# Moving two chunks of the shared expert's gate and up products into the last sequence's cross-attention of a decoder layer, with two smaller changes of order

## The chip, the cores and the metric

The kernel runs on one core of one Trainium2 chip. The metric is the device time of one execution in microseconds (us), as the median of several runs. All arithmetic is in 32-bit floats.

## The reference, cut to what matters

A decoder layer is applied to x of 8 sequences with 112 tokens and 512 features. Three blocks follow one another, each on a layer-normalised x and added to x:

```python
x = x + attn(layernorm(x), W_K, W_Q, W_V, W_O)       # 16 heads of 128, causal
x = x + xattn(layernorm(x), ctx_2048, Wq, Wk, Wv)    # 32 heads of 16, context of 375 per sequence
x = x + ffn(layernorm(x), gate_w, expert_*, shared_*)

# xattn: q = rmsnorm(x @ Wq.T by head), k = rmsnorm(ctx @ Wk.T by head), v = ctx @ Wv.T
#        out = softmax(q k^T / sqrt(16)) v
# ffn:   probs = softmax(x @ gate_w.T); the best 2 of 8 experts per token, their weights normed
#        out  = (silu(x @ shared_gate.T) * (x @ shared_up.T)) @ shared_down.T      # 704 wide
#        out += sum over the 2 experts e: w_e * (silu(x @ gate_e.T) * (x @ up_e.T)) @ down_e.T   # 352 wide
```

## The kernel before

The 896 tokens are held as 7 tiles of 128 rows (`xs`), with sequences 1 to 7 in the first 112 rows of a tile each and sequence 0 spread over the last 16 rows of all seven. The kernel has three stages, in this order: self-attention in four groups of heads, cross-attention, and the feed-forward part.

Code is traced in the order in which it stands, and a planner then gives each engine its own order. An engine runs its queue strictly in that order. The planner takes what stands first among the instructions that it holds to be ready, by costs of its own, so an instruction can float ahead of code that is written before it. Two helpers hold it: `tc.issue_after(i)` queues what is traced under it, on the engine of `i`, behind `i`; `tc.keep_in_program_order(i)` queues `i` behind what is already traced on its engine. Neither makes an engine wait for a result.

**Cross-attention before its loop.** `project_k` makes the raw keys of sequence 0. Seven tiles of x are normalised (`ln_apply`), projected to queries (`project_q`) and normed by head (`normed_q`). `project_q` ends in `head_squares`, a squaring on GpSimd (POOL, L407) and a sum on VectorE (DVE, L408). `normed_q` takes the square root on ScalarE (ACT, `rms_scale`, L411), multiplies on DVE (L523), turns the tile on TensorE (PE, L526) and copies it back on ACT (L527). `spread_q` (DVE, L533, two instructions per sequence) makes the operand of the scores from it. Two other jobs of POOL lie here: `weight_sums` (L454, four sums `wt` of weight blocks, the last two written into the query weights) and `chunk_sums(1)` (L471, four small sums of the next sequence's context). Both feed a product of 2 x 2 blocks with seven in place of eight multiplications (`first_chunks`, PE L476).

**The loop of cross-attention.** It runs over 8 sequences b, 2 halves of the heads cp and 3 thirds of the context m. `exp_scores` issues the scores of one (b, cp, m) into the four buffers of the PSUM pool `sc` (PE L569, tile `xs`) and four exponentials (ACT L577, tile `e`). `weigh` multiplies the exponentials of a half with the values (PE L594, tile `pv`), one half later. `attend(t)` turns and divides the result of a finished sequence and adds it to x. Between these, for b below 7, stand the products for the keys and values of sequence b+1. At the end of an iteration `spread_q`, `rms_scale` and `normed_k` (PE L551, ACT L554, tile `kT`) prepare b+1. Here `rms_scale` is held behind the exponentials of (b, 1, 1), so on ACT it stands between those and the exponentials of (b, 1, 2). Square root and exponential use different tables of ACT, and a load of the table (ACT_TABLE_LOAD) stands before the first instruction with another one. In iteration 5 the first four tiles of x, finished by then, are normalised and turned into `xn3`, the operand of the feed-forward part.

**The feed-forward part.** `shared_chunk(i, half, w)` makes 128 of the 704 gate and up rows (chunk i of 6) for half of the tokens: PE L722 (tile `gu`; gate and up are 8 matmul records each of 448 columns; chunk 5 has one such product), ACT L728 (Silu) and DVE L729. Its order is chunk (0, 0), the last three tiles of `xn3`, chunk (1, 0), `route`, and then the other ten. `route` computes the two experts of each token on DVE; POOL scatters the normalised rows to DRAM (L884), and `rows_of` loads them back sorted by expert (L914). 18 steps of experts follow, and `finish` adds the shared expert's down product. The weights of the shared expert are three tiles `sw`, two chunks in each, in the pool `weights` with three buffers, which the query, key and value weights of cross-attention hold before.

Of the kernel before, what the change touches and what calls it, by code (L numbers as in the profile page):

```python
# [15 lines left out]
F32 = mybir.dt.float32  # L16
I32 = mybir.dt.int32
AF = mybir.ActivationFunctionType
ALU = mybir.AluOpType
AX = mybir.AxisListType  # L20

P = 128
B, S, D = 8, 112, 512
NT = B * S
TT = NT // P
SP = P - S
ND = D // P
HALF = NT // 2
# [48 lines left out]
def decoder_layer(  # L77
    ctx: ExitStack, tc: tile.TileContext, x, ctxT, wqk, wv_all, wo, wx, wgate, wsgu, wsd, wegu, wed_a, wed_b, consts, out
):
    nc = tc.nc  # L80
# [6 lines left out]
    wpool = ctx.enter_context(tc.tile_pool(name="weights", bufs=3))  # L87
    mm = ctx.enter_context(tc.tile_pool(name="mm", bufs=4, space=PSUM))
# [28 lines left out]
    def psum(pool, name):  # L117
        return pool.tile([P, 512], F32, tag=pool.name, name=name)

    def load_w(pool, src, name):  # L120
        t = pool.tile([P, 4, 512], F32, tag="w", name=name)
        nc.sync.dma_start(out=t, in_=src)
        return t

    def load_ctx(b):
        t = ctxpool.tile([P, ND, M], F32, name=f"ctx{b}", tag="ctx")
        with tc.issue_after(first_weights):
            nc.sync.dma_start(out=t, in_=ctxT[b])
        return t


    def ln_begin(name):
# [251 lines left out]
    with ExitStack() as xa:  # L384
# [19 lines left out]
        def head_squares(n, dst, sums):  # L404

            sq = krp.tile([P, 512], F32, tag="sq", name="sq", bufs=2)
            nc.gpsimd.tensor_tensor(sq[:n], dst, dst, ALU.mult)  # L407
            nc.vector.tensor_reduce(sums, sq[:n].rearrange("p (h d) -> p h d", h=XH), AX.X, ALU.add)  # L408

        def rms_scale(t):  # L410
            nc.scalar.activation(t, t, AF.Sqrt, bias=eps_rms[: t.shape[0]], scale=1.0 / XD)  # L411
            nc.vector.reciprocal(t, t)
# [38 lines left out]
        def weight_sums(which):  # L451
            sums = ((wxv[:, 0:2], wxk[:, 0:2]), (wxv[:, 2:4], wt[0]), (wxv[:, 2:4], wxv[:, 0:2]), (wxk[:, 2:4], wt[1]))
            for i in which:
                nc.gpsimd.tensor_tensor(wt[i], *sums[i], ALU.subtract)  # L454
# [7 lines left out]
        def chunk_sums(b, which):  # L462
            a11, a12, a21, a22 = blocks(b)
            sums = (
                (a21, a22, ALU.add),
                (csum[0], a11, ALU.subtract),
                (a11, a21, ALU.subtract),
                (a12, csum[1], ALU.subtract),
            )
            for i in which:  # L470
                nc.gpsimd.tensor_tensor(csum[i], *sums[i])  # L471
# [30 lines left out]
        def project_q(t):  # L502
            q = qp.tile([P, 512], F32, tag="q", name="q")
            ss = qp.tile([P, XH], F32, tag="qss", name="qss")
            ps = psum(mm, "q")
            for c in range(ND):
                nc.tensor.matmul(
                    ps,
                    xn2[:, c, t * P : (t + 1) * P],
                    wxq[:, c, :],  # L510
                    start=(c == 0),
                    stop=(c == ND - 1),
                )
            nc.scalar.copy(q, ps)
            head_squares(P, q, ss)
            rawq[t] = (q, ss)

        def normed_q(t):

# [21 lines left out]
        def normed_k(b):  # L541
            k, kss = rawk.pop(b)
            keys[b] = kvp.tile([P, ND, M], F32, tag="kT2", name="kT2")
            for m in range(NM):
                k3 = k[:, m, :].rearrange("p (h d) -> p h d", h=XH)
                nc.vector.tensor_tensor(
                    k3, k3, kss[:, m, :, None].to_broadcast([MC, XH, XD]), ALU.mult
                )
                pt = psum(mm, "kT")
                for c in range(ND):  # L550
                    nc.tensor.transpose(  # L551
                        pt[:, c * MC : (c + 1) * MC], k[:, m, c * P : (c + 1) * P], ident[:MC, :MC]
                    )
                nc.scalar.copy(  # L554
                    keys[b][:, :, m * MC : (m + 1) * MC],
                    pt[:, : ND * MC].rearrange("p (c s) -> p c s", c=ND),
                )

        last_exp = {}

        def exp_scores(b, cp, m):

# [66 lines left out]
        new_keys(0)  # L629
        for m in range(NM):  # L630
            project_k(0, m)
        weight_sums((0, 1))
        for lo, hi in ((0, 4), (4, TT)):
            rs2 = ln_rstd(mv2, lo, hi)
            for t in range(lo, hi):
# [2 lines left out]
                    project_q(t - 1)  # L638
                if t >= 2:
                    normed_q(t - 2)  # L640
        project_q(TT - 1)
        normed_q(TT - 2)
        project_v(0, 0)
        rms_scale(rawk[0][1].rearrange("p m h -> p (m h)"))
# [2 lines left out]
        normed_q(TT - 1)  # L647
        spread_q(0)
        project_v(0, 2)
        weight_sums((2, 3))  # L650
        ctxs[1] = load_ctx(1)
        chunk_sums(1, range(4))

        pending = None
        for b in range(B):
            for cp in range(2):
                es = []
                for m in range(NM):
                    es.append(exp_scores(b, cp, m))
                    if m == 0 and pending is not None:  # L660
                        weigh(*pending)

                    if m == 1 and cp == 0 and b >= 2:
                        attend(b - 2)
                    if b + 1 < B:
                        if cp == 0:
                            if m == 0:
                                new_keys(b + 1)
                                pairs = first_chunks(b + 1)
                            next(pairs)  # L670
                        elif m == 0:
                            project_k(b + 1, 2)
                            if b + 2 < B:
                                ctxs[b + 2] = load_ctx(b + 2)
                                chunk_sums(b + 2, range(3))
                        elif m == 1:
                            project_v(b + 1, 2)
                        else:
                            next(pairs)
                            if b + 2 < B:  # L680
                                chunk_sums(b + 2, (3,))
                pending = (b, cp, es)
            if b + 1 < B:
                spread_q(b + 1)

                with tc.issue_after(last_exp[(b, 1, 1)].ins):
                    if b == 5:
                        rs3 = ln_rstd(mv3, 0, 4)
                    rms_scale(rawk[b + 1][1].rearrange("p m h -> p (m h)"))
                normed_k(b + 1)  # L690
                if b == 5:
                    for t in range(4):
                        ln_apply(mv3, rs3, t, xn3)
# [7 lines left out]
    with ExitStack() as ff:  # L701
# [5 lines left out]

        hidden = shp.tile([P, 6, NT], F32, name="hidden")
        wex = ep.tile([P, E, ND, 2 * FF], F32, name="wex")

        def load_shared(i):

            w = load_w(wpool, wsgu[i], f"sw{i}")
            return w.rearrange("p c (i k f) -> p c i k f", i=2, k=2)

        def shared_chunk(i, half, w):
            cols = bass.ds(half * HALF, HALF)
            both = []
            for k, pool in ((0, mm), (1, sc))[: 2 if i < 5 else 1]:
                ps = psum(pool, "gu")  # L720
                for c in range(ND):
                    nc.tensor.matmul(  # L722
                        ps[:, :HALF], w[:, c, i % 2, k, :], xn3[:, c, cols], start=(c == 0), stop=(c == ND - 1)
                    )
                both.append(ps[:, :HALF])
            g = gp.tile([P, HALF], F32, tag="g", name="g")
            if i < 5:
                nc.scalar.activation(g, both[0], AF.Silu)  # L728
                nc.vector.tensor_tensor(hidden[:, i, cols], g, both[1], ALU.mult)  # L729
                return  # L730


            n = P // 2
            gate, up = both[0][:n], both[0][n:]
            low = min(4 * P - half * HALF, HALF)
            nc.scalar.activation(g[:n, :low], gate[:, :low], AF.Silu)
            nc.vector.tensor_tensor(
                hidden[:n, i, half * HALF : half * HALF + low], g[:n, :low], up[:, :low], ALU.mult
            )
            if low < HALF:  # L740
                nc.scalar.activation(g[n:, low:], gate[:, low:], AF.Silu)
                nc.vector.tensor_tensor(hidden[n:, i, 4 * P :], g[n:, low:], up[:, low:], ALU.mult)
# [269 lines left out]
                    nc.vector.tensor_tensor(xs[t][:, cols], p[:, cols], xs[t][:, cols], ALU.add)  # L1012
                    nc.sync.dma_start(out=out[t * P : (t + 1) * P, cols], in_=xs[t][:, cols])

        sw = [load_shared(i) for i in range(3)]
        for e in range(E):
            nc.sync.dma_start(out=wex[:, e], in_=wegu[e])
        rs3b = ln_rstd(mv3, 4, TT)
        rs3s = [rs3] * 4 + [rs3b] * (TT - 4)
        shared_chunk(0, 0, sw[0])  # L1020
        for t in range(4, TT):
            ln_apply(mv3, rs3b, t, xn3)
        for t in range(6):
            normed_row(t)
        shared_chunk(1, 0, sw[0])
        at, share, expert = route()
        for i, half in ((0, 1), (1, 1), *((i, half) for i in range(2, 6) for half in range(2))):
            shared_chunk(i, half, sw[i // 2])

        thirds = [wpool.tile([P, 4, 512], F32, tag="w", name=f"wd{i}") for i in range(3)]  # L1030
# [117 lines left out]
```

## Time and profile before

| | |
|---|---|
| median of 3 runs | 1028.39 us (1027.58 to 1028.48) |
| profiled execution, its own time | 1028.71 us |
| its span, first to last instruction | 1026.9 us |
| PE busy in the span | 999.3 us, 97% |
| DVE, ACT, POOL busy | 39%, 27%, 24% |
| granted TensorE clock, mean | 0.998 |
| chain that ended last, PE's share | 91% |

All times inside the profile count from the start of its span; what lies outside the span is 1.8 us. A busy PE need not be at its peak: the records' ends are modelled, and a matmul that runs at a lower clock is as busy as another. So what PE loses is read from three things: its waits, the distance between the starts of equal matmuls, and the granted clock of a stretch.

| stretch, us | what runs | length, us | PE busy, us |
|---|---|---|---|
| 0 to 450.60 | load, self-attention | 450.6 | 437.8 |
| 450.60 to 506.85 | cross-attention up to the first scores | 56.25 | 53.33 |
| 506.85 to 740.83 | loop, sequences 0 to 6 | 233.98 | 229.15 |
| 740.83 to 762.05 | loop, sequence 7, up to the last turning | 21.22 | 20.11 |
| 762.05 to 834.33 | shared gate and up, routing | 72.28 | 72.28 |
| 834.33 to 983.00 | experts | 148.67 | 148.16 |
| 983.00 to the end | shared down, sums, output | 43.9 | 38.48 |

### The profile page before, as it was taken

How to read it: one execution, taken by the hardware profiler on the slowest of the kernel's cores; microseconds unless marked ns; L12 is line 12 of the kernel's file. 1: busy time of each engine (PE TensorE's matmuls, PEld its weight loads, DVE VectorE, ACT ScalarE, POOL GpSimd, SP SyncE). 2: the span in 40 equal slices, each digit the busy share in tenths (PEclk: the TensorE clock that was granted, in tenths of full speed). 3: DMA queues.
4: the chain of work that ended last, by engine and by line, in shares of the span. 5: the costliest groups of instructions: out<-in, count | busy, mean ns of one | idle time of the engine just before them, and what ended most of it. 6: DMA issues, size and time to landing. Idle time of an engine off the chain costs nothing.

```text
span 1026.9 us, 14752 instructions
## 1 busy us (share of the span) xinstructions
PE 999.3 (97%) x5732; PEld 532.4 (52%) x5732; DVE 397.7 (39%) x765; ACT 274.6 (27%) x514; POOL 248.7 (24%) x269
## 2 busy tenths in 40 slices
PE   5999999999999999999999999999999999999998
PEld 3556555554556455644455555555565544444433
DVE  3345224532345235546332443334334133333314
ACT  2122011210121002213354555445552111111200
POOL 3241034103411121152233312331224500000023
PEclk9999999999999999999999999999999999999999
DMA  9421012101200111000000101000328437777665
GB/s 343 190 86 47 0 42 83 49 1 41 82 18 34 41 41 48 4 1 0 31 31 2 32 31 32 14 20 1 124 105 363 176 116 226 233 233 232 211 196 166
DMA packets 31093, 95.66 MB, mean 93 GB/s; under 512 B 3888, under 2 KB 5808, under 8 KB 27440
## 3 DMA queue, kind: packets, MB, share of 16 engines
q1 hardware_dynamic: 25968, 82.11, 23.6%
q0 software_dynamic: 2320, 7.63, 2.3%
q10 hardware_dynamic: 2736, 4.98, 1.6%
q8 instruction: 46, 0.75, 0.3%
q14 instruction: 23, 0.19, 0.1%
HBM read 78.85 MB, written 14.94 MB: 91 GB/s over the span
## 4 chain that ended last, share of the span: by engine, by line
PE 91%; ACT 3%; DVE 3%; DMA 2%; POOL 1%; issue 0%; SPq 0%; DVEq 0%; ACTq 0%
PE qk L256 15%; PE v L333 9%; PE o L343 9%; PE kv L476 7%; PE gu L722 6%; PE xs L569 5%; PE gate L958 4%; PE y L980 4%; PE up L958 4%; PE pv L594 4%; PE k L417 3%; PE ys L1006 3%; PE xv L417 3%; PE z L221 2%; PE s L186 2%; ACT e L577 2%
## 5 line engine op out<-in xcount | busy, mean ns | idle before, releaser
L577 ACT ACTIVATE e<-xs 125x448 f32<-125x448 f32 x192 | 88.9, 549 | 67.1 <-PE xs L569 67.0
L333 PE MATMUL v<-w,xn 128*128 128x512 f32 x224 | 100.4, 594 | 0.0
L343 PE MATMUL o<-wo,zT 128*128 128x512 f32 x224 | 99.8, 594 | 0.0
L256 PE MATMUL qk<-xc,wc 128*128 128x448 f32 x180 | 70.1, 539 | 0.0
L722 PE MATMUL gu<-xn,sw 128*128 128x448 f32 x176 | 67.5, 540 | 0.0
L343 PEld LDWEIGHTS o<-wo,zT 128*128 128x128 f32 x224 | 41.0, 190 | 44.0 <-issue 43.8
L333 PEld LDWEIGHTS v<-w,xn 128*128 128x128 f32 x224 | 40.7, 190 | 42.1 <-issue 41.1
L207 POOL TENSOR_TENSOR s<-s,sm 112x448 f32<-112x448 f32 x32 | 30.2, 943 | 129.3 <-DVE sm L206 100.5
L991 POOL DMA_INDIRECT got<-routed,at x14 | 16.0, 1146 | 184.1 <-DMA routed<-y 180.1
L569 PE MATMUL xs<-qT,kT 32*125 32x224 f32 x768 | 54.6, 377 | 4.2 <-ACT kT L554 3.2
L958 PE MATMUL gate<-wex,xT 128*64 x144 | 55.3, 466 | 0.5 <-ACT xT L923 0.5
L569 PEld LDWEIGHTS xs<-qT,kT 32*125 32x125 f32 x768 | 36.0, 182 | 35.8 <-issue 27.5
L958 PE MATMUL up<-wex,xT 128*64 x144 | 54.3, 459 | 0.0
L256 PEld LDWEIGHTS qk<-xc,wc 128*128 128x128 f32 x180 | 34.2, 190 | 33.5 <-issue 32.3
L908 DVE COPY xn<-wex 128x704 f32 x60 | 31.2, 525 | 51.5 <-PE up L958 51.5
L256 PE MATMUL qk<-xn,w 128*128 128x448 f32 x120 | 50.2, 539 | 0.0
L980 PE MATMUL y<-wd,hT 128*64 128x512 f32 (+1 forms) x216 | 49.5, 592 | 0.6 <-ACT y L984 0.6
L722 PEld LDWEIGHTS gu<-xn,sw 128*128 128x128 f32 x176 | 32.9, 190 | 30.1 <-issue 30.1
L958 PE MATMUL gate<-xn,xT 128*64 128x352 f32 x120 | 45.9, 464 | 0.0
L958 PE MATMUL up<-xn,xT 128*64 128x352 f32 x120 | 45.3, 459 | 0.0
L350 DVE TENSOR_TENSOR x<-o,x 128x512 f32<-128x512 f32 x28 | 19.3, 689 | 60.7 <-PE o L343 60.6
L407 POOL TENSOR_TENSOR sq<-kraw 125x512 f32<-125x512 f32 x24 | 25.2, 1049 | 69.8 <-ACT kraw L440 37.3
(203 smaller groups left out, 1621.4 us busy)
## 6 DMA issues: line engine op xcount, KB each, us to landing
wd<-in_wed_a SPq DMA_DIRECT2D x27, 512.0 KB, 3.7
wex<-in_wegu SPq DMA_DIRECT2D x8, 1408.0 KB, 20.0
wd<-in_wed_b SPq DMA_DIRECT2D x36, 192.0 KB, 4.6
w<-in_wqk SPq DMA_DIRECT2D x6, 1024.0 KB, 4.8
ctx<-in_ctxT SPq DMA_DIRECT2D x8, 750.0 KB, 8.8
slots<-zeros SPq DMA_DIRECT2D x1, 4608.0 KB
wd<-in_wed_a SPq DMA_DIRECT2D x18, 256.0 KB, 4.6
routed<-y SPq DMA_DIRECT2D x18, 256.0 KB, 3.3
```

The costliest lines, as they stand in the source:

```text
L256: nc.tensor.matmul(ps[:, :HALF], wt[:, c * P : (c + 1) * P], x[:, c, :], start=(c == 0), stop=(c == 1))
L333: nc.tensor.matmul(ps, xn1[:, c, t * P : (t + 1) * P], wv[:, c, :], start=(c == 0), stop=(c == ND - 1))
L343: nc.tensor.matmul(ps, zT[:, h, t * P : (t + 1) * P], wog[:, h, :], start=(h == 0), stop=(h == GH - 1),)
L417: nc.tensor.matmul(ps[:MC, :], ctxs[b][:, c, m * MC : (m + 1) * MC], w[:, c, :], start=(c == 0), stop=(c == ND - 1),)
L476: nc.tensor.matmul(ps[:MC, :], x[:, c, :], w[:, c, :], start=(c == 0), stop=(c == 1))
L569: nc.tensor.matmul(strips[j][:MC, ci * 2 * S : (ci + 1) * 2 * S], keys[b][rows, 2 * cp + ci, m * MC : (m + 1) * MC], queries[b][rows, 2 * ...
L577: last_exp[(b, cp, m)] = nc.scalar.activation(e[:, :, j, :, :].rearrange("p c e s -> p c (e s)"), strips[j][:MC, : 4 * S].rearrange("p (c ...
L594: nc.tensor.matmul(ps[VW * j : VW * (j + 1), g * S : (g + 1) * S], v[:, m, 16 * cp + h, :], es[m][:, h // 8, (h % 8) // 2, h % 2, :], star ...
L722: nc.tensor.matmul(ps[:, :HALF], w[:, c, i % 2, k, :], xn3[:, c, cols], start=(c == 0), stop=(c == ND - 1))
L908: nc.vector.tensor_copy(second(j, c), wex[:, bass.ds(moved[j], 1), c, :].rearrange("p o f -> p (o f)"))
L958: nc.tensor.matmul(gu[k][n, :FF], xT[:, c, n], w, start=(c == 0), stop=(c == ND - 1))
L980: nc.tensor.matmul(ps[n, :], hT[:fn, i, n], w[i][:fn], start=(i == 0), stop=(i == len(FCH) - 1))
```

## The change

There are three edits.

1. **Weight sums.** `project_q` returns the squaring instruction of its tile, and all eight sums on POOL (`weight_sums((0, 1))`, `chunk_sums(1, ...)`, `weight_sums((2, 3))`) are now traced in one place, queued behind the squaring of the last tile of queries.
2. **Table.** After `rms_scale` of sequence b+1, an exponential of a single element is queued right behind the square root, in all seven iterations that have one. It is not used.
3. **Shared gate and up.** The gate and up products of chunks 0 and 1 for the first half of the tokens are computed inside iteration 7, one of the four products after each of (cp, m) = (0, 1), (0, 2), (1, 1), (1, 2) (`shared_ahead`). DVE copies them to a tile `ahead` in the weights' pool. `sw0` and `sw1` are loaded at the end of iteration 6, and `sw2` takes a buffer that is free later. In the feed-forward part, Silu and the multiplication read `ahead`; the chunks computed before and around the routing are now (2, 0) and (3, 0), and eight follow in place of ten.

```diff
@@ head_squares returns i.ins, project_q returns it as squared @@
+        warm = stp.tile([1, 1], F32, name="warm")
...
         for m in range(NM):
             project_k(0, m)
-        weight_sums((0, 1))
...
-        project_q(TT - 1)
+        squared = project_q(TT - 1)
         normed_q(TT - 2)
         project_v(0, 0)
...
         project_v(0, 2)
-        weight_sums((2, 3))
         ctxs[1] = load_ctx(1)
-        chunk_sums(1, range(4))
+
+        with tc.issue_after(squared):
+            weight_sums((0, 1))
+            chunk_sums(1, range(4))
+            weight_sums((2, 3))
+
+        def shared_ahead(i, k):
+            ps = psum(mm, "gu")
+            for c in range(ND):
+                nc.tensor.matmul(
+                    ps[:, :HALF], sw[0][:, c, i, k, :], xn3[:, c, :HALF], start=(c == 0), stop=(c == ND - 1)
+                )
+            nc.vector.tensor_copy(ahead[:, 2 * i + k, :HALF], ps[:, :HALF])
...
                             if b + 2 < B:
                                 chunk_sums(b + 2, (3,))
+                    elif m:
+                        shared_ahead(cp, m - 1)
...
                     rms_scale(rawk[b + 1][1].rearrange("p m h -> p (m h)"))
+                    tc.keep_in_program_order(nc.scalar.activation(warm, eps_rms[:1], AF.Exp))
                 normed_k(b + 1)
+                if b + 2 == B:
+                    sw = [load_shared(i) for i in range(2)]
+                    ahead = wpool.tile([P, 4, 512], F32, tag="w", name="ahead")
...
-        sw = [load_shared(i) for i in range(3)]
+        sw.append(load_shared(2))
         for e in range(E):
             nc.sync.dma_start(out=wex[:, e], in_=wegu[e])
         rs3b = ln_rstd(mv3, 4, TT)
         rs3s = [rs3] * 4 + [rs3b] * (TT - 4)
-        shared_chunk(0, 0, sw[0])
+        for i in range(2):
+            g = gp.tile([P, HALF], F32, tag="g", name="g")
+            nc.scalar.activation(g, ahead[:, 2 * i, :HALF], AF.Silu)
+            nc.vector.tensor_tensor(hidden[:, i, :HALF], g, ahead[:, 2 * i + 1, :HALF], ALU.mult)
+        shared_chunk(2, 0, sw[1])
...
-        shared_chunk(1, 0, sw[0])
+        shared_chunk(3, 0, sw[1])
         at, share, expert = route()
-        for i, half in ((0, 1), (1, 1), *((i, half) for i in range(2, 6) for half in range(2))):
+        for i, half in ((0, 1), (1, 1), (2, 1), (3, 1), (4, 0), (4, 1), (5, 0), (5, 1)):
             shared_chunk(i, half, sw[i // 2])
```

More of the change, by code (lines that the diff above doesn't have):

```diff
@@ L129, in load_ctx, with load_shared @@
         return t
+    def load_shared(i):
+        w = load_w(wpool, wsgu[i], f"sw{i}")
+        return w.rearrange("p c (i k f) -> p c i k f", i=2, k=2)
     def ln_begin(name):
@@ L406, in head_squares @@
             sq = krp.tile([P, 512], F32, tag="sq", name="sq", bufs=2)
-            nc.gpsimd.tensor_tensor(sq[:n], dst, dst, ALU.mult)
+            i = nc.gpsimd.tensor_tensor(sq[:n], dst, dst, ALU.mult)
             nc.vector.tensor_reduce(sums, sq[:n].rearrange("p (h d) -> p h d", h=XH), AX.X, ALU.add)
+            return i.ins
         def rms_scale(t):
@@ L514, in project_q @@
             nc.scalar.copy(q, ps)
-            head_squares(P, q, ss)
+            squared = head_squares(P, q, ss)
             rawq[t] = (q, ss)
+            return squared
         def normed_q(t):
@@ L709, in decoder_layer @@
         wex = ep.tile([P, E, ND, 2 * FF], F32, name="wex")
-        def load_shared(i):
-            w = load_w(wpool, wsgu[i], f"sw{i}")
-            return w.rearrange("p c (i k f) -> p c i k f", i=2, k=2)
         def shared_chunk(i, half, w):
```

## The prediction

> **What bounds the kernel now.** I read the page first, then the sums by stage, then who PE waits for, and last the timelines of the places that the diff touches.
>
> ```profile
> span 1026.9 us, 14752 instructions
> PE 999.3 (97%) x5732; PEld 532.4 (52%) x5732; DVE 397.7 (39%) x765; ACT 274.6 (27%) x514; POOL 248.7 (24%) x269
> ```
>
> PE bounds nearly everything, so what a change is worth is the PE time it takes away or fills. 27.6 us are idle, 9.8 of them at the start, far from the change. Stages (PE busy, PEld, DVE, ACT, POOL, granted clock, DMA share, GB/s):
>
> ```profile
> 740.83:762.05 21.22, 20.11 (x392) 15.56 (x392) 3.40 (x8) 13.31 (x27) 1.41 (x2) 0.92 0.11 45
> 762.05:834.33 72.28, 72.28 (x232) 37.84 (x231) 24.20 (x70) 12.57 (x20) 30.41 (x23) 1.00 0.61 238
> ...
> 750.00:753.50 3.50, 3.50 (x55) 2.91 (x58) 0.00 (x0) 1.85 (x4) 0.00 (x0) 0.52 0.00 0
> ```
>
> The shared stage has no idle PE at all. Sequence 7 looks 95% busy, but its clock is 0.92: from 750.0 to 753.5 TensorE had half its clock. PE's waits (total, times, longest):
>
> ```profile
> PE xs L569 <- ACT kT L554: 3.2, 6, 0.5
> PE qT L526 <- DVE q L523: 2.0, 2, 1.4
> PE xs L569 <- ACT e L577: 1.0, 2, 0.7
> PE xv L417 <- DVE v L444: 0.6, 1, 0.6
> ```
>
> Six waits of 0.54 are one per loop boundary; 1.4 and 0.6 lie at 493 and 499 us, where POOL sums weights; the 1.0 lies in sequence 7.
>
> **Edit 3, the tail.** What sequence 7 must do on PE, by the distances of starts in the chain: six `xs` groups of 0.97, three `pv` of 2.44, one turning of 1.02; 5.8 + 7.3 + 1.0 = 14.1 us. The stage lasts 21.2. So 7.1 us are lost: 1.0 as shown waits, 1.7 as the half clock (3.4 us at half rate), and the rest inside groups, whose matmuls trickle out as `xs` buffers come free:
>
> ```profile
> 746.23 2.05 PE L569 MATMUL xs<-qT,kT 32*125 32x224 f32 x16
> 748.61 2.99 PE L569 MATMUL xs<-qT,kT 32*125 32x224 f32 x16 [0.33 <-ACT e L577]
> 751.53 3.46 PE L594 MATMUL pv<-e,v 125*32 125x112 f32 x96
> ```
>
> The cause is ACT: four exponentials take 1.85 us, and the next scores wait for each buffer. The moved work is 4 products of 8 matmuls. The chain has 124 `gu` in 46.67 us, 0.376 each, so 32 cost 12.0 us. The shared stage loses 12.0. In sequence 7 the order as written, from its first score at 0, would be: `xs` to 1.0, `pv` of sequence 6 to 3.4, `xs` to 4.4, turning to 5.4, product to 8.4, `xs` to 9.4, product to 12.4, `xs` to 13.4, `pv` to 15.8, `xs` to 16.8, product to 19.8, `xs` to 20.8, product to 23.8, `pv` to 26.2. Each set of exponentials ends some 2 us after its `xs` (1.12 us to ACT's start, as from 744.24 to 745.35, then 1.85), always before PE needs it: those of the last `xs` at 22.8, needed at 23.8. So 12.0 in and 7.1 filled: the stage grows by 5.0, the next shrinks by 12.0: **-7.1 us**.
>
> A rule speaks of the clock here. The Trainium skill, page "TensorE: Matmul & The Clock Gate", section "HAM oscillation — how this bites in real kernels", asks only that PE has no gap over about 3.4 us. By that no gap of this stage (0.7 at most) would cost a clock, and filling would be worth 5.4. The row at 750.00 shows the drop at dense-looking 20.1 of 21.2 us; the trace decides, and I take 7.1. A PE without waits for 26 us should keep its clock, as it does in all other stages.
>
> What the move costs elsewhere:
> - Two Silu (0.54) and two multiplications (0.62) move with it; an extra table load of 1.28 falls where ACT waits 4.6 us for the last statistics. The multiplications share DVE with the last `attend`; the transposed tile 6 follows 0.28 us behind its input. I take 0.2, from 0 to 1.2.
> - Four copies `ahead` (0.62 each) fall on a DVE busy for 3.4 of 21.2 us: 0.
> - Loads: `sw0` and `sw1` take buffers read last at 724 and 731, and land in 4.7 us, long before. `sw2` (1 MB) waits on SP's queue for the last shared product, about 764, in front of the experts' eight loads, which wait for the last `pv` anyway; it is needed some 40 us later. The experts' weights start 4 to 5 us later and land in 20 to 24 us, some 30 before use: 0.
> - Cover: 12 us less work hides the routing. Sorted rows are fetched at 814.83 (two loads, 2.8 us to land), turned at 834.33: 16 us of slack, 4 are left. The first down weights go by the same SP queue, and `wd` in front of the rows waits for a weight buffer, chunk (3, 1) at the latest, near 808, before the scatters end: 0; without that cover, 1 us for each us that it is late.
>
> **Edit 2, the table.** At a boundary:
>
> ```profile
> 531.95 0.38 ACT L411 ACTIVATE kss<-kss,eps_rms 125x96 f32<-125x96 f32 x1
> 533.37 1.28 ACT L577 ACT_TABLE_LOAD   x1 [1.04 <-PE xs L569]
> 534.66 1.85 ACT L577 ACTIVATE e<-xs 125x448 f32<-125x448 f32 x4
> 536.37 1.57 ACT L554 COPY kT<-kT 128x500 f32<-128x500 f32 x3
> ...
> 537.03 1.04 PE L569 MATMUL xs<-qT,kT 32*125 32x224 f32 x16 [0.54 <-ACT kT L554]
> ```
>
> The exponential's table is loaded only when the scores are there. Ahead of them, it falls into the idle 1.04. The single element costs about 0.22 (the 64x64 Silu took 0.22). Exponentials then start near 533.6 instead of 534.66, end at 535.4, and the first key copy meets its transposes (done at 535.5) at once; PE goes on at 536.5, when its transposes end. All 0.54 go, six times: **-3.2 us**. What is late next is PE itself. The boundary after sequence 5 waits for DVE (`kraw`, `v`): 0.
>
> **Edit 1, the sums.** Now:
>
> ```profile
> 490.33 2.34 POOL L454 TENSOR_TENSOR wx<-wx 128x1024 f32<-128x1024 f32 x1 [0.53 <-PE q L507]
> 492.63 2.81 POOL L454 TENSOR_TENSOR wx<-wx,wt 128x1024 f32<-128x1024 f32 x1
> 495.41 1.04 POOL L407 TENSOR_TENSOR sq<-q 128x512 f32<-128x512 f32 x1
> ...
> 491.38 1.85 DVE L523 TENSOR_TENSOR q<-q,qss 128x512 f32<-128x512 f32 x1
> ```
>
> DVE's multiplication, 0.69 elsewhere, ends 0.56 after the POOL sum ends: it was shut out. With POOL empty, `qT` starts at 492.15 instead of 493.37 and the last squaring at 492.7 instead of 495.41, which also ends the 0.64 at 499: PE is 1.85 us ahead. But behind that squaring POOL now holds eight sums, 4 x 2.35 plus 4 x 0.65 = 12 us, to about 506. `spread_q(0)` on DVE (two of 0.37 to 0.45) comes near 502.3, and the first scores wait for both; PE would be there at 505.0. The skill's page "SBUF — State Buffer", section "Who interferes with whom", says that such a pair of DVE and POOL instructions excludes each other for a whole instruction, and the later one blocks. This trace agrees:
>
> ```profile
> 461.58 1.73 DVE L148 TENSOR_SCALAR xn<-x,mv,rs 128x512 f32<-128x512 f32 x2 [1.45 <-PE ln_t L155]
> ...
> 461.81 1.22 POOL L407 TENSOR_TENSOR sq<-kraw 125x512 f32<-125x512 f32 x1 [2.39 <-ACT kraw L440]
> ```
>
> Two such DVE instructions take 1.00 together with POOL idle (705.48); here POOL slipped in between and the second waited it out. So the first `spread_q` would wait for the third weight sum (503.7), the second for the fourth (506.2): scores at about 506.6, against 506.85 now. By the lock -0.25 is left of the 1.85 us; without it, all. Bounds: +1.0 (sums stretched to 2.81) and -1.9. I take **-0.3**, since the row at 461 is nearest.
>
> **Sum.** -7.1 + 0.2 - 3.2 - 0.3 = -10.4. The profiled execution took 1028.7 (span 1026.9 plus 1.8 outside it), 0.3 over the median; 1028.4 - 10.4 = **1018.0 us**.
>
> **The rivals.**
> - *The lock spares the spreads*: both DVE instructions pass together, edit 1 gives 1.85, 1016.4 us. For: the pair is issued back to back. Against: 461.58. Chance 15%.
> - *The tail fills by half*: operands of the shared products are ready from about 730, and the planner may pull them into waits that only its own costs see, or set ACT's order so that exponentials come late; 3.5 instead of 7.1, part of the half clock stays: 1021.6 us. For: a `memset` of the routing floated to 740.11. Against: written order has priority, and PE must do the work once, wherever. 20%.
> - *Slower: Silu among the last exponentials.* Its input is ready one `xs` before the next exponentials are, and no edge holds it. Each one placed there costs ACT two loads and itself, 1.28 + 1.28 + 0.54 = 3.1 us; queued ahead of exponentials that feed PE, while its product stands later in PE's queue, it adds a product, its eviction and copy, 3.0 + 1.1. Two cost 14.4; with 7.1 filled, 3.2 and 0.3 gained, +3.8: 1032.2 us. It decides from 5.2 us apiece. Against: `g` lies, in the memory map of this kernel, over the last of the four `e` buffers, free only after the last `pv`. 5%.
> - *Not what it says*: the planner's other shifts eat the gain, 1028: 3%. The change's own case keeps 57%.
>
> **The numbers.** 1018.0 is the likeliest case. The range 1015.0 to 1022.8 takes in the free lock, the half-filled tail and the bounds of edit 1, and leaves out the last two rivals and some of the edges. A measurement of this kernel tells 0.2% (2 us) from nothing: faster 0.92, same 0.03, slower 0.05.
>
> **What would show it.** Right: no PE wait of `xs` on `kT`; table loads straight behind L411; sequence 7 some 26 us long with a clock of 1.00; 60 us from its last turning to the experts in place of 72; `qT` without 1.4, and a wait of about 1.6 us before the first scores, with `spread_q` stretched beside L454. Wrong: Silu between exponentials, PE waiting for rows before the experts, or a second stretch at half clock.

## The result and the profile after

The changed kernel takes 1018.37 us (median of 6 runs, 1015.89 to 1020.43), the kernel before 1028.28 us (median of 6 runs beside them, 1027.28 to 1028.66). The ratio is 0.9902, with a 95% interval of 0.9886 to 0.9918. That is 9.9 us less.

The profiled execution of the changed kernel took 1016.08 us. The page begins:

```profile
span 1014.3 us, 14761 instructions
PE 991.4 (98%) x5732; PEld 527.0 (52%) x5732; DVE 401.9 (40%) x769; ACT 276.9 (27%) x522; POOL 246.6 (24%) x269
```

PE does the same 5732 matmuls as before. The two spans differ by 12.6 us, 2.7 more than the medians. The table below shows where: 2.3 us of it lie in the first 60 us, where nothing was changed. All lengths run from the start of one PE instruction to the start of another.

| stretch, us | before | after | difference | predicted |
|---|---|---|---|---|
| first product of self-attention to its first `v` | 48.33 | 46.03 | -2.30 | none |
| last `project_q` to the first scores (edit 1) | 18.48 | 17.97 | -0.51 | -0.3 |
| sequence 0 | 30.18 | 29.58 | -0.60 | -0.54 |
| sequence 1 | 32.62 | 32.05 | -0.57 | -0.54 |
| sequences 2, 3, 4, each | 33.45 | 32.88 | -0.57 | -0.54 |
| sequence 5 | 35.80 | 35.84 | +0.04 | 0 |
| sequence 6 | 35.03 | 34.43 | -0.60 | -0.54 |
| sequence 7 to the last turning | 21.22 | 26.76 | +5.54 | +5.0 |
| last turning to the router's product `lgT` | 14.37 | 15.05 | +0.68 | +0.2 |
| `lgT` to the first turned row of an expert | 57.91 | 45.88 | -12.03 | -12.0 |

Edit 1 gave 0.51 us, edit 2 gave 3.44 and edit 3 gave 5.81. Together these are 9.76 us, close to the 9.9 of the medians and to the 10.4 of the forecast.

Now the views that answer to those of before. The sums by stage (PE busy, PEld, DVE, ACT, POOL, granted clock, DMA share, GB/s), for sequence 7 and for the shared stage:

```profile
734.01:760.77 26.76, 26.76 (x425) 17.50 (x425) 5.91 (x13) 11.90 (x26) 1.41 (x2) 1.00 0.01 2
760.77:821.70 60.93, 60.63 (x202) 31.67 (x199) 24.00 (x70) 15.18 (x22) 30.09 (x23) 1.00 0.78 300
```

Sequence 7 has no idle PE left, and its clock is 1.00 where it was 0.92. The shared stage is shorter by what was taken out of it, and has one wait of 0.3.

Who PE waits for (total, times, longest):

```profile
PE xs L577 <- DVE qT L540: 1.5, 1, 1.5
...
PE ln_t L160 <- DVE v L505: 1.1, 1, 1.1
PE qT L533 <- DVE q L530: 0.8, 2, 0.6
```

The six waits of `xs` for the key copies `kT` are gone, and so is the wait of 1.0 for the exponentials. `qT` waits 0.8 in place of 2.0. One wait is new: 1.5 us of the first scores for `qT` on DVE. It is edit 1's, and comes up again below.

A loop boundary, ACT first and the next scores on PE after it (start, duration, then the idle time in front, where there is some):

```profile
528.56 0.37 ACT L417 ACTIVATE kss<-kss,eps_rms 125x96 f32<-125x96 f32 x1
528.95 1.28 ACT L713 ACT_TABLE_LOAD   x1
530.25 0.20 ACT L713 ACTIVATE warm<-eps_rms 1x1 f32<-1x1 f32 x1
530.36 1.79 ACT L585 ACTIVATE e<-xs 125x448 f32<-125x448 f32 x4
532.29 1.53 ACT L561 COPY kT<-kT 128x500 f32<-128x500 f32 x3
```

```profile
531.67 1.45 PE L558 MATMUL kT<-cst,kraw 125*128 125x125 f32 x12
533.04 1.04 PE L577 MATMUL xs<-qT,kT 32*125 32x224 f32 x16
```

The load runs in the time in which ACT used to wait for the scores. The exponentials follow it without a gap, and the scores of the next sequence start where the transposes end, with no bracket behind them.

Sequence 7 on PE, the second half of it:

```profile
742.41 1.04 PE L577 MATMUL xs<-qT,kT 32*125 32x224 f32 x16
743.38 3.27 PE L669 MATMUL gu<-xn,sw 128*128 128x448 f32 x8
746.59 1.04 PE L577 MATMUL xs<-qT,kT 32*125 32x224 f32 x16
747.55 2.51 PE L602 MATMUL pv<-e,v 125*32 125x112 f32 x96
749.99 1.04 PE L577 MATMUL xs<-qT,kT 32*125 32x224 f32 x16
750.96 3.27 PE L669 MATMUL gu<-xn,sw 128*128 128x448 f32 x8
```

The order is the written one, and every group has its plain length. Before, three of the six groups of scores lasted 2.05 to 2.99 us, since they trickled out behind the exponentials. A product takes 3.21 from its start to that of the scores behind it, where the forecast had 3.01.

### The profile page after: what moved, and what is told of

It is laid out like the page before. It is cut to its first block, busy times and chain, and to the rows that moved or that the text cites. A ratio compares the mean times of both kernels' runs of the same rounds, so it can differ in the third digit from the quotient of the medians.

```text
span 1014.3 us, 14761 instructions
## 1 busy us (share of the span) xinstructions
PE 991.4 (98%) x5732; PEld 527.0 (52%) x5732; DVE 401.9 (40%) x769; ACT 276.9 (27%) x522; POOL 246.6 (24%) x269
## 4 chain that ended last, share of the span: by engine, by line
PE 90%; issue 3%; DVE 3%; DMA 2%; POOL 1%; ACT 1%; SPq 0%; DVEq 0%; POOLq 0%; ACTq 0%
PE qk L261 16%; PE o L348 10%; PE v L338 10%; PE kv L482 9%; PE gu L744 5%; PE xs L577 5%; PE gate L980 4%; PE y L1002 4%; PE up L980 4%; PE pv L602 4%; PE ys L1028 3%; PE k L423 3%; PE xv L423 3%; PE z L226 2%; PE s L191 2%
## 5 line engine op out<-in xcount | busy, mean ns | idle before, releaser
L744 PE MATMUL gu<-xn,sw 128*128 128x448 f32 x144 | 55.5, 541 | 0.0
L577 PE MATMUL xs<-qT,kT 32*125 32x224 f32 x768 | 50.4, 373 | 1.5 <-DVE qT L540 1.5
L577 PEld LDWEIGHTS xs<-qT,kT 32*125 32x125 f32 x768 | 33.2, 181 | 32.5 <-issue 28.5
L271 ACT COPY p<-qk 128x448 f32<-128x448 f32 x15 | 8.0, 532 | 126.7 <-PE qk L261 126.7
L208 ACT ACTIVATE s<-s 112x448 f32<-112x448 f32 x32 | 18.5, 577 | 84.3 <-DVE s L207 78.9
```

Source lines behind the costliest of these rows:

```text
L577: nc.tensor.matmul(strips[j][:MC, ci * 2 * S : (ci + 1) * 2 * S], keys[b][rows, 2 * cp + ci, m * MC : (m + 1) * MC], queries[b][rows, 2 * ...
L744: nc.tensor.matmul(ps[:, :HALF], w[:, c, i % 2, k, :], xn3[:, c, cols], start=(c == 0), stop=(c == ND - 1))
```

## The experiments

The median of the kernel before was 1027.17 us beside e1 to e4, 1027.89 beside e5 to e8 and 1027.01 beside e9. The ratios are to the kernel before that ran on the same chip.

| kernel | median, us | ratio to before | 95% |
|---|---|---|---|
| e1, edit 1 alone | 1025.65 | 0.9983 | 0.9967 to 0.9999 |
| e2, edit 2 alone | 1024.75 | 0.9971 | 0.9958 to 0.9983 |
| e3, edit 3 alone | 1020.92 | 0.9940 | 0.9920 to 0.9959 |
| e4, two sums pinned | 1014.13 | 0.9880 | 0.9861 to 0.9899 |
| e5, Silu late | 1017.50 | 0.9890 | 0.9871 to 0.9909 |
| e6, e4 and e5 together | 1015.62 | 0.9869 | 0.9848 to 0.9891 |
| e7, Silu free to float | 1015.85 | 0.9892 | 0.9872 to 0.9911 |
| e8, e6 with four tiles turned later | 1013.38 | 0.9855 | 0.9835 to 0.9875 |
| e9, four tiles turned later alone | 1015.66 | 0.9880 | 0.9859 to 0.9900 |
| the changed kernel again, beside e9 | 1017.44 | 0.9902 | 0.9884 to 0.9919 |

Single runs of one kernel spread by 1.4 to 7.4 us; the profiles show two sources of it, the start-up and the clock (last section). The medians of the three edits alone are 1.5, 2.4 and 6.3 us under the kernel before; the stretches give 0.51, 3.44 and some 6, inside these intervals. So an effect below 2 us is read from the lengths of the stretches in the profiles. Where the code is the same and the clock was full, those used here repeat to 0.05 us.

**e1: edit 1 alone.** The kernel before, with the eight sums queued behind the last squaring.

```diff
         for m in range(NM):
             project_k(0, m)
-        weight_sums((0, 1))
...
         project_v(0, 2)
-        weight_sums((2, 3))
         ctxs[1] = load_ctx(1)
-        chunk_sums(1, range(4))
+
+        with tc.issue_after(squared):
+            weight_sums((0, 1))
+            chunk_sums(1, range(4))
+            weight_sums((2, 3))
```

> The kernel before with edit 1 alone (all eight sums of POOL behind the last squaring). Theory of the lock: the wait of 1.4 us at qT and of 0.64 at xv go, but spread_q (L533 of before, two instructions per sequence) is stretched to about 4.9 us for four, and PE waits about 1.5 us before the first scores; from the last project_q to the first scores 18.0 us in place of 18.48, so 0.5 us faster in all, about 1027.8. Rival (spread_q passes between the sums): no wait before the first scores, 16.5 us, about 1026.4. Rival (other work floats to new places): the loop or the tail changes by more than 0.3 us.

The stretch went from 18.48 to 17.97, as in the changed kernel. DVE's four records of `spread_q` (two for sequence 0, two for sequence 1), in the kernel before and then in e1, with the scores behind them:

```profile
504.20 1.54 DVE L533 TENSOR_SCALAR qT<-xn,cst 128x448 f32<-128x448 f32 x4 [0.42 <-ACT xn L527]
```

```profile
498.67 4.87 DVE L535 TENSOR_SCALAR qT<-xn,cst 128x448 f32<-128x448 f32 x4 [0.42 <-ACT xn L529]
502.87 1.04 PE L571 MATMUL xs<-qT,kT 32*125 32x224 f32 x16 [1.48 <-DVE qT L535]
```

Beside them POOL ran its last two weight sums back to back:

```profile
497.77 2.35 POOL L455 TENSOR_TENSOR wx<-wx 128x1024 f32<-128x1024 f32 x1
500.07 2.49 POOL L455 TENSOR_TENSOR wx<-wx,wt 128x1024 f32<-128x1024 f32 x1
```

The four DVE records take 1.54 in the kernel before and 4.87 here. They do not pass together. Taken singly, the first lasts 1.69 and ends 0.24 behind the third weight sum, the second lasts 2.53 and ends 0.26 behind the fourth, and the other two take 0.44 each. So PE reaches the scores earlier and then waits 1.48. The rival in which the lock spares the spreads is out.

**e4: only two of the sums pinned.** The changed kernel, with `weight_sums((0, 1))` back in its old place, behind the keys' products, and the small sums free.

```diff
         for m in range(NM):
             project_k(0, m)
+        weight_sums((0, 1))
...
         with tc.issue_after(squared):
-            weight_sums((0, 1))
-            chunk_sums(1, range(4))
             weight_sums((2, 3))
+        chunk_sums(1, range(4))
```

> The changed kernel, but only the last two weight sums (those that overwrite the query weights) stay behind the last squaring; the other six sums go back to where they were before, during the last output projection. Theory of the lock: POOL is empty from about 496 us, spread_q takes 1.5 us for four, PE does not wait before the first scores, 1.5 us faster than the changed kernel, about 1016.9. Rival (spread_q is late for another reason, such as ACT's copy behind the table load): the wait of 1.5 us stays and the time is that of the changed kernel, 1018.4.

```profile
490.48 2.35 POOL L460 TENSOR_TENSOR wx<-wx 128x1024 f32<-128x1024 f32 x1
492.79 2.81 POOL L460 TENSOR_TENSOR wx<-wx,wt 128x1024 f32<-128x1024 f32 x1
```

```profile
498.90 1.54 DVE L540 TENSOR_SCALAR qT<-xn,cst 128x448 f32<-128x448 f32 x4 [0.42 <-ACT xn L534]
501.56 1.04 PE L577 MATMUL xs<-qT,kT 32*125 32x224 f32 x16
```

POOL is done at 495.6, before the spreads start. They take 1.54 again, the scores wait for nothing, and the stretch is 16.42: 1.55 less than in the changed kernel and 2.06 less than before. The old collision therefore cost at least 2.06 us. The changed kernel gets a quarter of it, because it moves the collision from one DVE instruction to another.

**e2: edit 2 alone.**

```diff
+        warm = stp.tile([1, 1], F32, name="warm")
...
                     rms_scale(rawk[b + 1][1].rearrange("p m h -> p (m h)"))
+                    tc.keep_in_program_order(nc.scalar.activation(warm, eps_rms[:1], AF.Exp))
```

> The kernel before with edit 2 alone (the exponential of one element behind each square root). Theory: each of six loop boundaries shortens by 0.57 to 0.60 us, the one after sequence 5 by nothing, so 3.4 us faster, about 1024.9; no PE wait of xs on kT is left. Rival (the wait only changes hands, from kT to the exponentials or to DVE): below 1 us gained, above 1027.3. The half clock in sequence 7 should still be there, since its waits on ACT are untouched.

Sequences 0 to 4 lasted 29.58, 32.05 and three times 32.88, sequence 6 34.42; sequence 5 stayed at 35.84. These are the changed kernel's lengths to 0.01. Edit 2 is worth 3.44 us by itself and does not depend on the others.

**e3: edit 3 alone.** The kernel before, with `shared_ahead`, the early loads and the new order of the chunks.

> The kernel before with edit 3 alone (four shared products in sequence 7). Theory: sequence 7 takes 26.8 us in place of 21.2 from its first scores to the last turning, at full clock; from there to the router 15.0 in place of 14.4; from the router to the experts 45.9 in place of 57.9: 5.8 us faster, about 1022.5. Rival (what is gained is mostly the clock): with the half clock gone but the waits only moved, 1.7 us, about 1026.6. Each product should cost 3.2 us in place of 3.0, since a change from 32-row to 128-row tiles and back stands around it.

Sequence 7 lasted 26.76, the next stretch 14.78 and the one after it 45.88: 6.1 us less than before in these three (87.42 against 93.50). Sequences 5 and 6, which this edit does not touch, were longer than before by 0.5 and 2.7 in the profiled run: TensorE ran at half clock there, from the boundary that follows sequence 5 on.

```profile
703.40:710.20 6.80, 6.80 (x54) 4.99 (x56) 1.09 (x2) 3.83 (x8) 0.00 (x0) 0.50 0.01 2
```

```profile
701.24 0.62 PE L556 MATMUL kT<-cst,kraw 125*128 125x125 f32 x4 [0.53 <-DVE kraw L551]
702.93 1.58 PE L160 MATMUL ln_t<-cst,xn 128*128 128x128 f32 x8 [1.07 <-DVE v L504]
```

**e5: Silu and its multiplications late.** In the changed kernel the two multiplications `hidden<-g,ahead` share DVE with the last `attend`. Here they are held behind the transposed tiles.

```diff
-        for i in range(2):
-            ... Silu and multiplication of ahead
         shared_chunk(2, 0, sw[1])
         for t in range(4, TT):
-            ln_apply(mv3, rs3b, t, xn3)
+            turned_last = ln_apply(mv3, rs3b, t, xn3)      # returns its copy on ACT
+        with tc.issue_after(turned_last.ins):
+            for i in range(2):
+                ... Silu and multiplication of ahead
```

> The changed kernel, with the Silu and multiplication of the two chunks of ahead queued on ACT behind the last copy into xn3, so that they no longer stand between the last attend and the last statistics on DVE. Theory: the 0.67 us that the stretch from the last turning to the router grew by (15.05 in place of 14.37) comes from those two multiplications, so 14.4 here, 0.65 us faster than the changed kernel. Rival (the stretch grew by the change between 32-row and 128-row tiles, or by the order of the chunks): 15.0 stays. The load of sw2, which waits for the buffer of ahead, comes some 6 us later and holds the experts' loads behind it back; it should cost nothing, as they land over 20 us before use.

In the changed kernel, with the last turning at 760.77, DVE did:

```profile
763.21 0.62 DVE L1045 TENSOR_TENSOR hidden<-g,ahead 128x448 f32<-128x448 f32 x1 [0.30 <-ACT g L1044]
763.75 0.42 DVE L632 TENSOR_TENSOR t<-o_t,r 128x256 f32<-128x256 f32 x1
764.09 0.61 DVE L1045 TENSOR_TENSOR hidden<-g,ahead 128x448 f32<-128x448 f32 x1
765.32 0.69 DVE L142 BATCH_NORM_STATS2 st<-x 128x6 f32<-128x512 f32 x1 [0.62 <-POOL x L634]
```

In e5, with the last turning at 763.71:

```profile
765.89 0.42 DVE L632 TENSOR_TENSOR t<-o_t,r 128x256 f32<-128x256 f32 x1
767.15 0.69 DVE L142 BATCH_NORM_STATS2 st<-x 128x6 f32<-128x512 f32 x1 [0.84 <-POOL x L634]
```

The statistics start 3.44 us after the last turning in e5 and 4.55 in the changed kernel. The stretch to `lgT` is 14.37, what it was before edit 3. So the work that e5 moves is the whole of the 0.68. It moves Silu and its table load too, but these were not late in the changed kernel: ACT had loaded the next table and waited 1.32 for the statistics from DVE.

```profile
763.66 1.28 ACT L147 ACT_TABLE_LOAD   x1
766.26 0.30 ACT L147 ACTIVATE rs<-mv,eps_ln 128x3 f32<-128x3 f32 x1 [1.32 <-DVE mv L143]
```

What is left are the two multiplications, the first of which waited for Silu (0.30) with the last `attend` behind it. The median, 1017.50, moved by less than the runs spread (1014.83 to 1018.30). Two of the five runs had a mean clock of 0.997, and the profile of one of them shows the half clock behind sequence 5.

**e6: e4 and e5 together.**

> Both repairs in one kernel: only the last two weight sums behind the last squaring, and the Silu of ahead behind the last copy into xn3. Theory: the gains add, 1.55 + 0.65 = 2.2 us faster than the changed kernel by the stretches of the profile: 16.4 us from the last project_q to the first scores, 26.8 for sequence 7, 14.4 to the router, 45.9 to the experts. About 1013.5 us where the start and the clock are undisturbed. Rival (they share a cause): 1.5 or less.

The stretches were 16.42 and 14.37: the two gains add. Together they are 2.23 us by stretch; the median was 1015.62, with a start-up that was 2.0 us longer than in the profile of the changed kernel.

**e7: Silu free to float.** What the forecast held against the rival in which Silu comes between the last exponentials was the memory of `g`, which lies over an `e` buffer. Here Silu's result goes to a buffer that is free early.

```diff
-            g = gp.tile([P, HALF], F32, tag="g", name="g")
+            g = lnpool.tile([P, D], F32, tag="xn", name="xn")[:, :HALF]
```

> The changed kernel, with the buffer of Silu of ahead taken from the pool of normalised rows, which is free during sequence 7, in place of one that lies over the exponentials' buffers. The planner then places one Silu before the exponentials of (7, 0, 2) and one before those of (7, 1, 2), each with two loads of the table. Theory of the prediction's slower rival in its mild form: each costs ACT 3.1 us, of which PE waits for 1 to 2, and may bring a half clock back, so sequence 7 takes 29 to 31 us in place of 26.8, 2 to 4 us slower than the changed kernel, about 1021. In the prediction's own full form (7.2 us each): sequence 7 over 40 us, above 1032. Rival (ACT has room for all of it): 26.8 stays.

The planner did what the rival says, twice. The first time on ACT:

```profile
740.18 1.28 ACT L1044 ACT_TABLE_LOAD   x1
742.96 0.58 ACT L1044 ACTIVATE xn<-ahead 128x448 f32<-128x448 f32 x1 [1.50 <-DVE ahead L672]
743.56 1.28 ACT L585 ACT_TABLE_LOAD   x1
744.85 1.85 ACT L585 ACTIVATE e<-xs 125x448 f32<-125x448 f32 x4
```

The scores that needed these buffers are the ones at 746.37. They took 1.40 in place of 1.04, and that is all PE lost:

```profile
746.37 1.40 PE L577 MATMUL xs<-qT,kT 32*125 32x224 f32 x16
```

Sequence 7 lasted 27.13 (+0.37), and the way to `lgT` 14.71 (-0.34). The mechanism is real, and its price is next to nothing here. That the products which edit 3 put between the scores give ACT the room for it is argued from the lengths and was not tested.

**e8: e6, with the four finished tiles turned inside iteration 6.** They were normalised and turned at the boundary that follows sequence 5, where PE waits 0.53 and 1.07 us.

```diff
                     elif m:
                         shared_ahead(cp, m - 1)
+                    if b == 6 and 0 < 3 * cp + m < 5:
+                        ln_apply(mv3, rs3, 3 * cp + m - 1, xn3)
...
                 normed_k(b + 1)
-                if b == 5:
-                    for t in range(4):
-                        ln_apply(mv3, rs3, t, xn3)
```

> Both repairs as in e6, and the four tiles of xn3 that are normalised and turned at the boundary after sequence 5 are turned one by one inside iteration 6. Theory: the profile of edit 3 alone showed TensorE at half clock for 6.8 us from that boundary on, where PE waits 0.5 us for kraw and 1.1 us for v; runs of a mean clock near 0.996 are those. Without these waits the boundary after sequence 5 shortens by up to 1.6 us and no run has a clock below 0.998, so about 1012 with a narrower spread. Rival (the drop is not tied to that boundary): clocks of 0.995 to 0.996 stay in a fifth to a third of the runs.

```profile
696.77 0.62 PE L558 MATMUL kT<-cst,kraw 125*128 125x125 f32 x4 [0.52 <-DVE kraw L553]
697.32 1.04 PE L577 MATMUL xs<-qT,kT 32*125 32x224 f32 x16
```

The wait of 1.07 for `v` is gone with the transposes that stood behind it. Sequence 5 lasted 33.66 in place of 35.84, sequence 6 34.76 in place of 34.43. All four runs had a clock of 1.0. This version has the lowest median: 1013.38 us, 0.9855 of the time before. Its interval overlaps that of e4.

**e9: only that move, on the changed kernel, beside the changed kernel again.**

> The changed kernel with one difference: the four tiles of x that are finished at the end of iteration 5 are normalised and turned inside iteration 6, one after each of four steps, in place of all four at the loop's boundary. Theory (the boundary with its transposes and two waits is what sends TensorE to half clock in some runs): the boundary after sequence 5 goes from 35.84 to 33.7 us, iteration 6 grows by 0.3, together -1.8 us; the half clock of 6.8 us that about a third of the changed kernel's runs show is in none of these, so the slowest runs vanish too: all clocks 0.999 or 1.0, median 2 to 3 us under the changed kernel's, near 1015.5. Rival (the sums pinned in two places, which the earlier version of this move also had, kept the clock): clock 0.996 stays in a third of the runs; only the 1.8 us are gained.

> The changed kernel unaltered, on the same chip as the version that turns the four tiles later. Both theories: 1015.9 to 1020.4, clock 0.996 in about a third of the runs (two of six before).

Sequence 5 lasted 33.67 and sequence 6 34.76, the same 1.84 us less. The medians differ by 1.78 (1015.66 and 1017.44). On the question of the clock the pair says nothing: all five runs of e9 had 0.999, but all six of the changed kernel had 1.0, so the half clock that was to vanish did not appear in this pair at all.

## Why the prediction was right, step by step

The forecast was 1018.0 us, and 1018.37 was measured. The mechanism of each edit came out as it was worked out. The terms of edits 1 and 2 lie within 0.3 us of their forecasts; edit 3 was over-estimated by 1.1. That the totals lie only 0.37 us apart is luck in part: edits 1 and 2 gave 0.45 more than forecast, which hides some of the 1.1, and single runs of the changed kernel spread by 4.5 us.

- **Edit 2: -3.2 forecast, -3.44 measured**, in the changed kernel and in e2. All of the 0.54 went, at six boundaries, and PE was late next, as worked out. The forecast's start of the exponentials left out the 0.22 that it had given the single element; in the trace they start 0.13 behind the load. The rest of the gain, 0.03 to 0.06 per boundary, was not separated.
- **Edit 1: -0.3 forecast, -0.51 measured.** The reading of the row at 461 held, and so did the order worked out from it: the first `spread_q` waited for the third weight sum and the second for the fourth. PE's wait of 1.5 before the first scores is the 1.6 of the forecast. e4 shows the other side: without sums beside the spreads, the stretch is 2.06 shorter, near the 1.85 that the forecast gave to a free lock.
- **Edit 3: -6.9 forecast (-7.1 and 0.2), -5.81 measured.** The filling worked as the written order said: all 26.76 us of sequence 7 are busy, and the shared stage shrank by 12.03 for a forecast of 12.0. Two terms were mis-sized. The stage grew by 5.54 and not by 5.0, since the four products took 12.71 us in place of 12.03 between the scores (3.10, 3.21 and twice 3.20; where this lies is in the last section). And "I take 0.2" for the work that moves with Silu was 0.68 (0.41 in e3), within the bounds given (0 to 1.2); e5 and ACT's wait of 1.32 show that it is the two multiplications in front of the last `attend`, not the table load.
- **The half clock in the tail: 1.7 of the 7.1.** It is gone: the profiles of the kernel before, e1 and e2 show it, and none of the nine profiles with edit 3 does. In the 85 runs without edit 3 (53 of the kernel before, e1 and e2) the mean clock was 0.998 or less in all but one; 3.4 us at half clock make 0.998. In the 47 runs with edit 3, it was 0.999 or 1.0 in 39, and 0.996 or 0.997 in the other 8. The rule of the Trainium skill that the forecast weighed (page "TensorE: Matmul & The Clock Gate", section "HAM oscillation — how this bites in real kernels") would have valued the filling at 5.4. 12.71 us of products went in and the stage grew by 5.54, so 7.17 were filled: the trace's 7.1, not the rule's 5.4.
- **"A second stretch at half clock"** was named as a sign of being wrong. Such a stretch shows in 2 of the changed kernel's 12 runs, as a mean clock of 0.996. e3 and e5, whose profiles caught one, place it behind sequence 5 and not in the tail. The two runs were the slowest of the first six (1019.09 and 1020.43). The clock of the six runs of the kernel before beside them is not on record, so what it did to the comparison is not known.
- **The loads.** `sw0` and `sw1` went out at 718.32. `sw2` waited until 764.73, between the first and the second of the experts' loads, not in front of all eight:

```profile
761.00 0.33 SPq L1039 DMA_DIRECT2D wex<-in_wegu  x1
764.73 0.33 SPq L122 DMA_DIRECT2D sw<-in_wsgu  x1
765.11 4.65 SPq L1039 DMA_DIRECT2D wex<-in_wegu  x7
```

The forecast took `sw2`'s buffer to be the one that the last shared product reads; it is that of `ahead`, freed by the second multiplication at 764.70. The time is the same, 764, and nobody waited. The sorted rows were fetched at 813.91 and turned at 821.70, so with the 2.8 us of landing taken off, as in the forecast, some 5 us of the 16 are left where 4 were forecast.

- **The rivals.** The free lock is refuted by e1, the half-filled tail by sequence 7's 26.76 of 26.76. Silu among the exponentials did not happen in the changed kernel. e7 made it happen, and the two together cost 0.4 us at most where the forecast said 14.4. The step that failed there is "queued ahead of exponentials that feed PE, while its product stands later in PE's queue": the first Silu needs `ahead`, which was ready at 742.96, and the exponentials behind it were needed only at 746.4. So the reason that the forecast gave for the small chance of 5%, the buffer under `g`, was not what kept the kernel fast: without it, next to nothing was lost.

## What to carry to other kernels

Where a stage is full of short waits because one engine feeds another in small steps, independent work from a later, fully busy stage can fill it. Here it was worth what the stage lost, its clock included, less what the added work itself delayed; the loss is read from the distances between starts and the granted clock, not from the busy share. Pinning work of POOL to another place gains in full only if that place has no DVE instruction on the path (0.51 against 2.06 us here): look for the next pair that collides, and move no more of it than has to move. A table that ACT needs can be loaded by an instruction of one element, put where ACT waits anyway.

## What the runs showed of the hardware

**Half clock without a gap.** In the kernel before, TensorE fell to half clock in the tail for 3.4 us with no gap over 0.7 us in the stage. Behind sequence 5, the profiles of e3 and e5 show it for 6.8 us, after gaps of 0.53 and 1.07. It is not in every run. The mean clock of a run does not tell the place, but it was 0.996 or 0.997 in 8 of 38 runs of versions with edit 3 that keep this boundary, and in none of the 9 runs of e8 and e9. Without edit 3 it was 0.992 to 0.996, lower than the 0.998 that the tail alone makes, in 20 of the 53 runs of the kernel before and in 10 of the 32 of e1 and e2; no profile caught one of these. Nine runs are too few to call it removed: at a rate of 8 in 38, nine runs without it have a chance of about 1 in 8. In the traces' record of the granted clock, every length between two changes is a whole multiple of 3.41 us (6.83 is two of them, and the 730.45 before the drop in the tail are 214). So in these traces the clock changes on a grid of 3.41 us; what decides at each step stays open.

**The start-up differs by 2 us from run to run.** The same 16 matmuls at the start of self-attention, in the profile of before and in that of after:

```profile
14.52 8.82 PE L311 MATMUL qk<-xn,w 128*128 128x448 f32 x16 [0.68 <-ACT xn L156]
```

```profile
14.35 6.28 PE L316 MATMUL qk<-xn,w 128*128 128x448 f32 x16 [0.68 <-ACT xn L161]
```

At 0.376 us from start to start, as elsewhere, 16 matmuls take 6.0. In the first row 7 of them take 5.2 us, 0.74 each, as at half clock. The traces' record of full clock begins at 19.67 in the kernel before and at 13.24 in the changed one. The stretch around these matmuls was 45.8 to 48.3 us over twelve profiles, with no relation to the version: it was 45.8 to 46.1 in the six where that record begins before 14.0, and 47.3 to 48.3 in the six where it begins after 17.0. A pair of profiled spans can therefore differ by 2 us for reasons that have nothing to do with the change, and here did.

**A shared product between scores costs 0.1 us more at each end.** Scores use 32 rows of the array, shared products 128. In a product that stands between scores, the first of the eight matmuls is 0.48 from the second, and the last is 0.47 from the scores that follow (from `pv` in the fourth product); the others keep 0.376. The four products have seven such ends, since the first of them follows the turned tile and starts with 0.378: seven times 0.1 is the 0.7 us that the forecast lacked. That the change of shape is the reason was not tested, and the 0.48 stands also at 14.35, in front of which PE was idle.
